# Layernorms with a full-matrix variance and a root on all partitions; the gelus of a feed-forward issued together

## The chip, the cores and the metric

The kernel runs on one core of one Trainium2 chip. The metric is the time of one execution on the device, in microseconds (us). A profile of one execution is at hand: it lists every instruction with its start and its length on each engine. The engines are TensorE (PE for matmuls, PEld for weight loads), VectorE (DVE), ScalarE (ACT), GpSimd (POOL) and SyncE (SP), which only issues DMAs here.

## What is computed

All data are fp32. The input x is 8 batches of 256 positions with 128 features; ctx is a second input of the same shape. The reference does, in short:

```
x1 = LN(x + ssm(x))            # LN, up-projection, conv of 4, silu, scan over 16 states, gate, down-projection
x2 = LN(x1 + cross(x1, ctx))   # layernorms, 16 heads of 64, softmax
x3 = x2
for 6 layers:
    x3 = x3 + attention(shift_tokens(x3))   # 16 heads of 64, windows of 32, normalised q and k, rotary tables
    x3 = x3 + ffn(shift_tokens(x3))         # LN(g, b); W1 128 -> 2 x 341; a * gelu(gate) @ W2
out = LN(x2 + x3)
LN(x) = (x - mean(x)) / sqrt(var(x) + 1e-5), over the 128 features, with g and b in some places
```

## The kernel before

Features lie on the 128 partitions and positions on the free axis. Two batches make a pair of 512 columns (`TP`), and there are four pairs. A matrix product on fp32 data runs as two passes on TensorE, so the profile counts two MATMUL records for each call. The kernel has three stages, one after the other, and a tail:

- Stage 1 (0 to 405 us of the span): the scan block, pair by pair. A generator `pre` prepares pair p + 1 (its layernorm included) while `scan` works on pair p.
- Stage 2 (405 to 770): cross-attention, pair by pair, with layernorms of the context, of x1 and of the result.
- Stage 3 (770 to about 2509): six layers of window attention and feed-forward.
- The tail, to 2556.5: the last feed-forward, then four final layernorms one after the other, and the stores.

There are 48 layernorms of 128x512: 8 in stage 1, 12 in stage 2, 24 in stage 3 (one in each feed-forward) and 4 in the tail. All go through the generator `layernorm_steps`: the mean by one product with `mean_w`, a full 128x128 matrix of 1/128 (L104); `ln_xc` = x - mean on VectorE (L106); `ln_sq` = its square on ScalarE (L108); then a `yield`. Next comes the variance (L112): four products in which a 128-column block of `ln_sq` is the weight and one column of `mean_w` the moving operand, so that the variances of 512 positions land as 128x4, one position per partition. `inv_root` takes Ln (with 1e-5 as bias) and then Exp with the scale -0.5 on ScalarE, both on 128x4 (`ln_rs`, L89, the line of the helper). After a second `yield`, four products spread the roots over the partitions (`ln_bc`, L122): each has a column of `ln_rs`, repeated 128 times, as its weight and the identity as moving operand. VectorE multiplies `ln_xc` by `ln_bc` (L127, or L129 and L130 with g and b).

PSUM is taken from pools with two buffers for each tag: `big` is 128x1024, `s` and `o` are 128x512. The pool of the layernorms' tiles has two buffers as well.

ScalarE must have the right table of functions loaded. `load_table` (L93) loads the one that holds Ln and Exp and keeps that instruction in program order; `with_table` makes Ln and Exp follow it. Other functions such as gelu load their table where they first stand in ScalarE's order.

In stage 3 the order of TensorE's instructions is the order in which the program is written (`tc.manual_schedule` for that engine alone). The order on the other engines is chosen by the framework's scheduler when the program is built, within data dependencies and `tc.issue_after` hints.

The written order comes from a list `slots` that is run through once for each batch of a layer (a turn). A turn has four groups. Each group begins with `turn_weights` (pT_ps, L730, with its copy pT on ScalarE, L734), and then has `project_out` (y_ps, L774, and x, L779, on VectorE) in groups 1 and 3, or `value` (v_ps by the products of L602, with its copy on ScalarE, L639) in groups 2 and 4; `attend` (o_ps, L742, and `on`, L749, on VectorE); `scores` (s_ps, L699; mask added on VectorE, L707; max, L712; subtraction on POOL, L713; Exp on ScalarE is `weigh`); `add_weights` (sum and reciprocal on VectorE, L722 and L723); `root` (max of `ss` on VectorE, L634, then Ln and Exp to `rn` on ScalarE); `turn` (qkT_ps, L652, copied by ScalarE to qT, L659, or kz, L664); `turn_output` (oT_ps, L761, copied by ScalarE, L765); `query_key` (qk_ps, L602; `sq` on ScalarE, L614; `qk`, `rb` and `ss` on VectorE, L621, L622 and L626; an addition on POOL, L625); `normalise` (POOL, L645). `spread` issues the DMAs of `vz` on SP.

A feed-forward of a pair (two batches) is a generator too. It is advanced by one step at each slot marked "ff": four slots in an even turn and four in an odd one. These steps have names in what follows:

- E1: shifted copies `fxs` on ScalarE (L793, L794).
- E2: the layernorm's mean, `ln_xc`, `ln_sq`.
- E3: variance and root.
- E4: `ln_bc` and the two operations that make `fxn` on VectorE.
- O1: `up(1)`, three products to f_ps (L808): the first two share a buffer of the tag `big`, the third takes one of `s`. Gelus 1 and 2 (L821).
- O2, right behind `turn_weights` of group 2: gelu 3 and `load_table`.
- O3: `up(0)` (again L808) and `fh` on VectorE (L827).
- O4: `down`, three products to f2_ps (L833), and x on VectorE (L834).

There are 24 feed-forwards. Between O1 and O3, tag `big` is used by qkT_ps, f_ps, qk_ps and v_ps, in this order, through two buffers, so v_ps of group 2 takes the buffer of f_ps, and may write only once gelus 1 and 2 have read it.

Of the kernel before, what the change touches and what calls it, by code (L numbers as in the profile page):

```python
# [9 lines left out]
FP = mybir.dt.float32  # L10
AF = mybir.ActivationFunctionType
ALU = mybir.AluOpType
AX = mybir.AxisListType

P = 128
# [34 lines left out]
def decoder_kernel(ctx: ExitStack, tc: tile.TileContext, a: dict, out: bass.AP):  # L50
    nc = tc.nc
    V, A, G, T = nc.vector, nc.scalar, nc.gpsimd, nc.tensor
# [3 lines left out]
    lnp = ctx.enter_context(tc.tile_pool(name="lnp", bufs=2))  # L56
# [5 lines left out]
    def ps_big(name):  # L62
        return banks[-1].tile([P, 1024], FP, tag="big", name=name)

    def ps_s(name):
        return banks[-1].tile([P, 512], FP, tag="s", name=name)
# [4 lines left out]
    ident = keep.tile([P, P], FP, name="ident")  # L71
# [3 lines left out]
    mean_w = keep.tile([P, P], FP, name="mean_w")  # L75
    G.memset(mean_w, 1.0 / D)
    eps_t = keep.tile([P, 1], FP, name="eps_t")
    G.memset(eps_t, EPS)

    def col(name, i=0, n=P):  # L80
        o = _OFF[name] + i
        return cols[:n, o : o + 1]

    table = []

    def with_table(f, *args, **kw):

        with tc.issue_after(table[-1].ins) if table else ExitStack():
            return f(*args, **kw)  # L89

    def load_table():
        table.append(
            tc.keep_in_program_order(A.preload_act_table_set("natural_log_exp_and_others"))  # L93
        )

    def inv_root(dst, src, bias=0.0):

        with_table(A.activation, dst, src, AF.Ln, bias=bias)
        with_table(A.activation, dst, dst, AF.Exp, scale=-0.5)

    def layernorm_steps(x, dst, g=None, b=None, view=lambda t: t):

        mu = ps_s("ln_mu")
        T.matmul(mu, lhsT=mean_w, rhs=x, start=True, stop=True)  # L104
        xc = lnp.tile([P, TP], FP, name="ln_xc")
        V.tensor_tensor(xc, x, mu, ALU.subtract)  # L106
        sq = lnp.tile([P, TP], FP, name="ln_sq")
        A.activation(sq, xc, AF.Square)  # L108
        yield
        var = ps_s("ln_var")  # L110
        for j in range(4):
            T.matmul(  # L112
                var[:, j : j + 1], lhsT=sq[:, j * P : (j + 1) * P], rhs=mean_w[:, 0:1],
                start=True, stop=True,
            )
        rs = lnp.tile([P, 4], FP, name="ln_rs")
        inv_root(rs, var[:, 0:4], eps_t)
        yield

        bc = ps_s("ln_bc")  # L120
        for j in range(4):
            T.matmul(  # L122
                bc[:, j * P : (j + 1) * P], lhsT=rs[:, j : j + 1].to_broadcast([P, P]), rhs=ident,
                start=True, stop=True,
            )
        if g is None:
            V.tensor_tensor(dst, xc, bc, ALU.mult)  # L127
        else:
            V.scalar_tensor_tensor(dst, view(xc), g, view(bc), ALU.mult, ALU.mult)  # L129
            V.tensor_scalar(dst, dst, b, None, ALU.add)  # L130

    def layernorm(*args):
        for _ in layernorm_steps(*args):
            pass
# [27 lines left out]
    with (  # L162
# [29 lines left out]
        def decay():  # L192
            with_table(A.activation, aa, cols[:, _OFF["a_log"] : _OFF["a_log"] + 2 * NS], AF.Exp)
            V.tensor_scalar(aa, aa, -1.0, None, ALU.mult)
            V.reciprocal(ia, aa)
            i_ps = ps_s("i_ps")
            for h in range(2):
                T.transpose(i_ps[:NS, h * P : (h + 1) * P], ia[:, h * NS : (h + 1) * NS], ident)
            A.copy(iaT.rearrange("n h p -> n (h p)"), i_ps[:NS, : 2 * P])
# [3 lines left out]
        for h in range(2):  # L203
            r_ps = ps_s("tap_ps")
            for k in range(KC):
                T.matmul(
                    r_ps[:, k * P : (k + 1) * P],
                    lhsT=col("conv_w", h * KC + k).to_broadcast([P, P]), rhs=ident,
                    start=True, stop=True,
# [16 lines left out]
        def pre(p, got, t_in=None):  # L226
# [7 lines left out]
            yield  # L234
            xn = xns[p % 2][:, :, KC - 1 :]
            yield from layernorm_steps(x, xn, col("ssm_g"), col("ssm_b"), two)
            yield
            xm, gate, dt = [], [], []
# [153 lines left out]
    with tc.tile_pool(name="s2w", bufs=1) as wp, tc.tile_pool(name="s2", bufs=2) as sp:  # L392
# [10 lines left out]
        def project(p, got):  # L403

            ct = sp.tile([P, TP], FP, name="ct")
            load_transposed(a["ctx_1024"], p, ct, sp)
            cn = sp.tile([P, TP], FP, name="cn")
            yield from layernorm_steps(ct, cn, col("ctx_w"), col("ctx_b"))
            yield
            la = sp.tile([P, TP], FP, name="la")  # L410
# [80 lines left out]
        for p in range(NPAIR):  # L491
# [13 lines left out]
            for hb in range(NHB):  # L505
                T.matmul(
                    y_ps, lhsT=wo[:, hb, :], rhs=oT[:, hb, :], start=(hb == 0), stop=(hb == NHB - 1)
# [7 lines left out]
    with ExitStack() as st:  # L515
# [270 lines left out]
        def feed_forward(d, p):  # L786

            w1, w2 = wts[d][1:3]
            x = x3[p]
            xs = sp.tile([P, 2, S], FP, name="fxs", bufs=1)  # L790
            x4 = x.rearrange("p (b s) -> p b s", b=2)
            G.memset(xs[HD:, :, 0:1], 0.0)
            A.copy(xs[:HD], x4[:HD])  # L793
            A.copy(xs[HD:, :, 1:], x4[HD:, :, : S - 1])  # L794
            xn = sp.tile([P, TP], FP, name="fxn", bufs=1)
            yield
            yield from layernorm_steps(
                xs.rearrange("p b s -> p (b s)"), xn, col("ff_g", d), col("ff_b", d)
            )
            yield  # L800
            hh = sp.tile([P, 3, TP], FP, name="fh", bufs=1)

            def up(i):

                pr, p2 = ps_big("f_ps"), ps_s("f_ps")
                got = []
                for dst, (f0, n) in zip((pr[:, :TP], pr[:, TP:], p2), FB):
                    T.matmul(  # L808
                        dst[:n], lhsT=w1[:, i * DFF + f0 : i * DFF + f0 + n], rhs=xn,
                        start=True, stop=True,  # L810
                    )
                    got.append(dst[:n])
                return got

            gts = []
            for j, g in enumerate(up(1)):
                n = FB[j][1]
                if j == 2:
                    yield
                gt = sp.tile([P, TP], FP, name="fg", bufs=3)  # L820
                A.activation(gt[:n], g, AF.Gelu, bias=col("ff_b1", d * 6 + 3 + j, n))  # L821
                gts.append(gt)
            load_table()
            yield
            for j, v in enumerate(up(0)):
                n = FB[j][1]
                V.scalar_tensor_tensor(  # L827
                    hh[:n, j, :], v, col("ff_b1", d * 6 + j, n), gts[j][:n], ALU.add, ALU.mult
                )
            yield  # L830
            y_ps = ps_s("f2_ps")
            for j, (f0, n) in enumerate(FB):
                T.matmul(y_ps, lhsT=w2[:n, j, :], rhs=hh[:n, j, :], start=(j == 0), stop=(j == 2))  # L833
            V.scalar_tensor_tensor(x, y_ps, col("ff_b2", d), x, ALU.add, ALU.add)  # L834
            yield
# [28 lines left out]
        def run(n):  # L864
            nonlocal ff
            for f, k, *args in slots:
                if f == "ff":
                    if k == n % 2:
                        next(ff, None)
                elif 0 <= n + k < len(seq):  # L870
                    f(n + k, *args)
                    if f is project_out and k < 0 and seq[n + k][1] % 2:
                        ff = feed_forward(seq[n + k][0], seq[n + k][1] // 2)
# [6 lines left out]
        with tc.manual_schedule(engines={mybir.EngineType.PE}):  # L880
            shift(0)
            for n in range(-2, len(seq)):
                run(n)
            project_out(len(seq) - 1, 1)
            for _ in feed_forward(DEPTH - 1, NPAIR - 1):
                pass
# [90 lines left out]
```

## Time and profile before

| | |
|---|---|
| Time, three runs | 2563.87, 2559.03, 2560.82 us; median 2560.82 |
| Profiled execution | 2558.4 us, its span 2556.5 us |
| PE busy | 2342.5 us, 92% of the span |
| PEld busy | 1469.9 us, 57% |
| DVE busy | 1800.3 us, 70% |
| ACT busy | 1468.3 us, 57% |
| POOL busy | 1428.2 us, 56% |
| DMA | 154.62 MB |
| granted TensorE clock, mean | 0.954 of full speed |

The span runs from the first to the last instruction in the profile; the execution's own time also has what lies before and after. Busy times of different engines overlap. A matmul's busy time may hold some waiting in TensorE's pipeline, and PEld overlaps PE. In lines of the profile, `a<-b,c 128x512` is the output, the inputs and the tile; `x8` counts records that are folded into one line; `[0.17 <-ACT pT L734]` is idle time of the engine ahead of the instruction and what ended it. The chain that ended last is followed back from the last instruction, at each step to what released it.

### The profile page before, as it was taken

The numbers are of one execution on the slowest core, as the hardware profiler recorded it, in microseconds if no ns is written. First come the engines' busy times: TensorE is split into PE (matmuls) and PEld (weight loads), VectorE is DVE, ScalarE is ACT, GpSimd is POOL, SyncE is SP. The second block draws the span as 40 slices with busy tenths as digits, with TensorE's granted clock in tenths as the row PEclk, the third lists the DMA queues.
The fourth block names the chain that finished last, engine by engine and source line by source line (L and its number), as shares of the span: only waits on it lengthen the run. The fifth ranks groups of instructions, "written<-read, shape, count | busy, mean of one in ns | idle before, by whom it ended". The sixth has DMA issues, their size and how long they took to land.

```text
span 2556.5 us, 54468 instructions
## 1 busy us (share of the span) xinstructions
PE 2342.5 (92%) x21378; PEld 1469.9 (57%) x21378; DVE 1800.3 (70%) x2671; ACT 1468.3 (57%) x2392; POOL 1428.2 (56%) x1174
## 2 busy tenths in 40 slices
PE   7687777999978999999999999999999999999996
PEld 3233224555445666666666666666666666666664
DVE  5777782544358778777778778777788777777762
ACT  4443422544435666666666666666666666666652
POOL 4877781322237655566656666566656656666630
PEclk8887877999989999999999999999999999999997
DMA  3433331000022223322232223222232223222220
GB/s 105 101 84 91 92 91 50 1 1 1 1 76 55 64 55 73 73 63 56 59 78 66 64 59 73 69 66 57 57 80 65 64 57 73 56 57 56 57 56 17
DMA packets 437962, 154.62 MB, mean 60 GB/s; under 512 B 401294, under 2 KB 417548, under 8 KB 437580
## 3 DMA queue, kind: packets, MB, share of 16 engines
q1 hardware_dynamic: 437708, 151.14, 24.4%
q8 instruction: 171, 2.80, 0.5%
q14 instruction: 83, 0.68, 0.1%
HBM read 55.33 MB, written 1.31 MB: 22 GB/s over the span
## 4 chain that ended last, share of the span: by engine, by line
DVE 27%; PE 26%; ACT 13%; POOL 1%; issue 1%; DMA 1%; SPq 1%; ACTq 0%; DVEq 0%; POOLq 0%
DVE qk L621 6%; DVE rb L622 6%; DVE ss L626 6%; PE qk_ps L602 5%; PE f_ps L808 3%; DVE on L749 3%; PE o_ps L742 3%; PE f_ps L833 2%; ACT sq L614 2%; PE qkT_ps L652 2%; DVE mx L722 2%; ACT kz L664 2%; PE s_ps L699 2%; PE oT_ps L761 2%; PE v_ps L602 2%; ACT pw L89 2%
## 5 line engine op out<-in xcount | busy, mean ns | idle before, releaser
L625 POOL TENSOR_TENSOR qk<-qk,rb 128x512 f32<-128x512 f32 x384 | 480.8, 1273 | 433.4 <-DVE rb L622 287.2
L645 POOL TENSOR_TENSOR qk<-qk,rn 128x1024 f32<-128x1024 f32 x192 | 369.0, 1922 | 31.0 <-ACT rn L89 28.7
L621 DVE TENSOR_TENSOR qk<-qk_ps,tab 128x1024 f32<-128x1024 f32 x192 | 234.8, 1223 | 204.2 <-ACT sq L614 204.2
L602 PE MATMUL qk_ps<-wqkv,xs 128*128 128x512 f32 x768 | 370.1, 605 | 7.3 <-issue 3.4
L713 POOL TENSOR_TENSOR pw<-pw,mx 128x512 f32<-128x512 f32 x192 | 200.1, 1042 | 160.5 <-DVE mx L712 106.8
L664 ACT COPY kz<-qkT_ps 64x1024 f32<-64x1024 f32 x192 | 193.4, 1007 | 118.5 <-PE qkT_ps L652 113.3
L742 PE MATMUL o_ps<-vz,pT 128*32 128x128 f32 x6144 | 207.5, 276 | 29.9 <-ACT pT L734 27.1
L626 DVE TENSOR_REDUCE ss<-sq 128x16 f32<-128x1024 f32 x192 | 232.0, 1208 | 3.2 <-ACT sq L614 3.2
L622 DVE TENSOR_TENSOR rb<-qk_ps,tab 128x1024 f32<-128x1024 f32 x192 | 233.0, 1214 | 1.4 <-POOL qk L625 1.4
L307 PE MATMUL y<-mc,ident 128*128 128x512 f32 x256 | 170.3, 768 | 66.5 <-POOL mc L326 63.3
L722 DVE TENSOR_REDUCE mx<-pw 128x8 f32<-128x512 f32 x192 | 130.6, 680 | 140.7 <-ACT pw L89 138.5
L461 POOL TENSOR_TENSOR ws<-w 128x512 f32<-128x512 f32 x64 | 81.3, 1270 | 259.7 <-ACT w L89 178.7
L742 PEld LDWEIGHTS o_ps<-vz,pT 128*32 128x32 f32 x6144 | 156.0, 109 | 118.4 <-ACT pT L734 107.5
L659 ACT COPY qT<-qkT_ps 128x1024 f32<-128x1024 f32 x96 | 97.2, 1012 | 218.5 <-PE qkT_ps L652 218.0
L614 ACT ACTIVATE sq<-qk_ps 128x1024 f32<-128x1024 f32 x192 | 195.3, 1017 | 41.2 <-PE qk_ps L602 35.0
L652 PE MATMUL qkT_ps<-ident,qk 128*128 128x128 f32 x1536 | 210.2, 280 | 7.3 <-POOL qk L645 4.3
L324 DVE TENSOR_TENSOR_SCAN m<-dw,ab 128x256 f32<-128x256 f32 x256 | 161.9, 670 | 59.5 <-POOL mc L326 37.8
L699 PE MATMUL s_ps<-kz,qT 128*32 128x128 f32 x6144 | 202.9, 273 | 0.6 <-ACT kz L664 0.6
L326 POOL TENSOR_TENSOR mc<-m,rows 128x512 f32<-128x512 f32 x128 | 167.9, 1318 | 53.2 <-PE d_ps L267 28.1
L602 PEld LDWEIGHTS qk_ps<-wqkv,xs 128*128 128x128 f32 x768 | 133.4, 194 | 104.4 <-issue 101.0
L652 PEld LDWEIGHTS qkT_ps<-ident,qk 128*128 128x128 f32 x1536 | 165.2, 141 | 48.3 <-issue 41.6
L774 PE MATMUL y_ps<-oT,wo 128*128 128x128 f32 x1536 | 187.7, 275 | 1.5 <-DVE ln_xc L106 0.9
(152 smaller groups left out, 4425.5 us busy)
## 6 DMA issues: line engine op xcount, KB each, us to landing
vz<-v SPq DMA_DIRECT2D x1152, 64.0 KB, 2.2
rows<-bc_dram SPq DMA_DIRECT2D x128, 256.0 KB, 3.7
vz<-v SPq DMA_DIRECT2D x576, 32.0 KB, 2.2
wqkv<-in_L_ffn_Wqkv SPq DMA_DIRECT2D x18, 512.0 KB, 4.7
wo<-in_L_ffn_Wo SPq DMA_DIRECT2D x6, 512.0 KB, 7.9
w<-in_L_ffn_W SPq DMA_DIRECT2D x6, 341.0 KB, 3.4
t_in<-in_x SPq DMA_DIRECT2D x4, 256.0 KB, 2.9
wkv<-in_L_xattn_Wkv SPq DMA_DIRECT2D x1, 1024.0 KB
```

The source lines that it names most:

```text
L602: T.matmul(pr[:, i * 512 : (i + 1) * 512], lhsT=got[n]["xs"][:, tb * P : (tb + 1) * P], rhs=thirds[seq[n][0], c][:, i * 512 : (i + 1) * 51 ...
L614: A.activation(sq, p3, AF.Square)
L621: V.tensor_tensor(t, p3, cs, ALU.mult)
L622: V.tensor_tensor(rb, p3, sn, ALU.mult)
L625: G.tensor_tensor(t[:, :, o], t[:, :, o], rb[:, :, f], ALU.add)
L626: V.tensor_reduce(got[n]["ss"][:, 2 * c + tb, :], sq, AX.X, ALU.add)
L645: G.tensor_tensor(t, t, r, ALU.mult)
L652: T.transpose(t_ps[:, hb * P : (hb + 1) * P], t[:, 2 * hb : 2 * hb + 2, :].rearrange("p h d -> p (h d)"), ident,)
L664: A.copy(kzs[0][r, :, e, W + tb * P : W + (tb + 1) * P], t3[r])
L699: T.matmul(s_ps[i * W : (i + 1) * W, j * P : (j + 1) * P], lhsT=qT[:, 4 * g + i, j * W : (j + 1) * W], rhs=kz[:, 4 * g + i, :, k0 : k0 + 2 ...
L713: G.tensor_tensor(pw, pw, mx[:, 0].unsqueeze(3).to_broadcast(shape), ALU.subtract)
L742: T.matmul(o_ps[i * W : (i + 1) * W, j * P : (j + 1) * P], lhsT=pT[:, j, i * W : (i + 1) * W], rhs=vz[:, j, i].rearrange("p e d -> p (e d) ...
```

## The change

The variance is one product with the full matrix `mean_w`, so that all 128 partitions hold the variance of each position, in a tile of 128x512. `inv_root` runs on that whole tile (Ln from PSUM into `ln_sq`, Exp in place), and `ln_bc` is gone: VectorE multiplies `ln_xc` by `ln_sq`. In `feed_forward`, the `yield` that stood ahead of gelu 3 stands ahead of gelu 1, so that all three gelus are written in step O2. They are issued through a new helper, `other_table`, which puts each behind the last four activations that went through `with_table` in ScalarE's order. The generator has as many steps as before.

```diff
-    table = []
+    table, recent = [], []
     def with_table(f, *args, **kw):
         with tc.issue_after(table[-1].ins) if table else ExitStack():
+            recent.append(f(*args, **kw))
+            return recent[-1]
+
+    def other_table(f, *args, **kw):
+        with ExitStack() as st:
+            for i in recent[-4:]:
+                st.enter_context(tc.issue_after(i.ins))
             return f(*args, **kw)
...
         A.activation(sq, xc, AF.Square)
         yield
         var = ps_s("ln_var")
-        for j in range(4):
-            T.matmul(
-                var[:, j : j + 1], lhsT=sq[:, j * P : (j + 1) * P], rhs=mean_w[:, 0:1],
-                start=True, stop=True,
-            )
-        rs = lnp.tile([P, 4], FP, name="ln_rs")
-        inv_root(rs, var[:, 0:4], eps_t)
+        T.matmul(var, lhsT=mean_w, rhs=sq, start=True, stop=True)
+        inv_root(sq, var, eps_t)
         yield
-        bc = ps_s("ln_bc")
-        for j in range(4):
-            T.matmul(
-                bc[:, j * P : (j + 1) * P], lhsT=rs[:, j : j + 1].to_broadcast([P, P]), rhs=ident,
-                start=True, stop=True,
-            )
         if g is None:
-            V.tensor_tensor(dst, xc, bc, ALU.mult)
+            V.tensor_tensor(dst, xc, sq, ALU.mult)
         else:
-            V.scalar_tensor_tensor(dst, view(xc), g, view(bc), ALU.mult, ALU.mult)
+            V.scalar_tensor_tensor(dst, view(xc), g, view(sq), ALU.mult, ALU.mult)
             V.tensor_scalar(dst, dst, b, None, ALU.add)
...
             for j, g in enumerate(up(1)):
                 n = FB[j][1]
-                if j == 2:
+                if j == 0:
                     yield
                 gt = sp.tile([P, TP], FP, name="fg", bufs=3)
-                A.activation(gt[:n], g, AF.Gelu, bias=col("ff_b1", d * 6 + 3 + j, n))
+                other_table(A.activation, gt[:n], g, AF.Gelu, bias=col("ff_b1", d * 6 + 3 + j, n))
                 gts.append(gt)
             load_table()
             yield
```

## The prediction

> **What bounds the kernel now.** I read the page first, then the busy time by stage, then ScalarE's and TensorE's timelines over one period of the window-attention stage, then the chain that ended last.
>
> ```profile
> span 2556.5 us, 54468 instructions
> ...
> PE 2342.5 (92%) x21378; PEld 1469.9 (57%) x21378; DVE 1800.3 (70%) x2671; ACT 1468.3 (57%) x2392; POOL 1428.2 (56%) x1174
> ...
> DVE 27%; PE 26%; ACT 13%; POOL 1%; issue 1%; DMA 1%; SPq 1%; ACTq 0%; DVEq 0%; POOLq 0%
> ```
>
> PE is busy 92% of the span, yet the chain has as much VectorE as TensorE in it: the bound alternates. Busy time by stretch (columns: stretch, length, then PE, PEld, DVE, ACT, POOL busy with counts, clock, DMA share, GB/s):
>
> ```profile
> 860.00:2480.00 1620.00, 1562.33 (x17797) 1084.52 (x17796) 1263.69 (x1891) 1063.72 (x1747) 979.02 (x781) 1.00 0.27 64
> ...
> 1492.96:1564.73 71.77, 69.38 (x790) 48.11 (x789) 55.74 (x84) 47.45 (x78) 43.83 (x36) 1.00 0.24 56
> ```
>
> Stage 3 is 24 feed-forwards at about one per 71.8 us (E1 to E4, O1 to O4, as named above); 22 of them run in this steady state. In the chain, O3, O4 and E1 go through PE without a gap; E2 to O1 go through sq -> qk, rb, ss on DVE and back through ACT. So a cycle gets longer wherever either link does. ScalarE's timeline across O1 and O2 (start, length, instruction, idle before it):
>
> ```profile
> 1548.54 1.28 ACT L821 ACT_TABLE_LOAD   x1
> 1549.83 1.26 ACT L821 ACTIVATE fg<-f_ps,cols 128x512 f32<-128x512 f32 x2
> 1550.98 0.58 ACT L765 COPY oT<-oT_ps 128x512 f32<-128x512 f32 x1
> 1551.45 0.70 ACT L821 ACTIVATE fg<-f_ps,cols 85x512 f32<-85x512 f32 x1
> 1552.03 1.02 ACT L614 ACTIVATE sq<-qk_ps 128x1024 f32<-128x1024 f32 x1
> 1552.93 0.59 ACT L734 COPY pT<-pT_ps 128x512 f32<-128x512 f32 x1
> 1553.55 1.28 ACT L93 ACT_TABLE_LOAD   x1
> ```
>
> Today sq waits behind all three gelus, although its input left PE at about 1551.3. TensorE's timeline, same stretch:
>
> ```profile
> 1537.98 1.06 PE L122 MATMUL ln_bc<-ident,ln_rs 128*128 128x128 f32 x8
> 1538.87 0.60 PE L761 MATMUL oT_ps<-ident,on 128*128 128x128 f32 x4
> ...
> 1551.09 0.60 PE L730 MATMUL pT_ps<-ident,pw 128*128 128x128 f32 x4
> 1551.52 1.88 PE L602 MATMUL v_ps<-wqkv,xs 128*128 128x512 f32 x4
> 1553.58 1.08 PE L742 MATMUL o_ps<-vz,pT 128*32 128x128 f32 x32 [0.17 <-ACT pT L734]
> ...
> 1557.22 0.66 PE L761 MATMUL oT_ps<-ident,on 128*128 128x128 f32 x4 [0.57 <-DVE on L749]
> ...
> 1559.43 0.60 PE L730 MATMUL pT_ps<-ident,pw 128*128 128x128 f32 x4
> ```
>
> v_ps starts right behind pT_ps: the slot it takes, that of up(1)'s first two products, is free because gelus 1 and 2 ended at 1551.09. Last, the chain in the tail, where each layernorm stands alone:
>
> ```profile
> 2536.72 1.88 PE ln_var L112 x8
> ...
> 2538.62 0.27 ACT ln_rs L89
> ...
> 2539.18 2.08 PE ln_bc L122 x8
> 2541.26 1.72 PE ln_mu L104 x2
> ```
>
> **What the Trainium skill says.** "PSUM — Partial Sum Buffer", section "Engine vs sequencer instructions": ScalarE's and VectorE's queues are strict FIFO and matmuls start in program order; the timelines agree (sq idle behind the gelus). The same page, "PSUM bank collisions raise a hardware error": two engines on one bank get a dependency, ACT and DVE too; that is why DVE's qk waited 204.2 us in all on ACT's sq. "TensorE: Matmul & The Clock Gate", "What's actually happening": after an idle window the array runs at half clock; here ln_mu takes 1.02 us at 1520.23 and 2.07 at 218.87.
>
> **The change, part by part.** 48 layernorms.
>
> *Variance.* Removed per layernorm: 8 ln_var passes and 8 ln_bc passes; 0.91 + 0.89 us of PE in steady state (start to start), 1.88 + 2.08 where PE is cold. Added: two passes of 512 columns, priced by ln_mu, which has the same form: 0.86 warm, 2.07 cold.
>
> *Root.* Removed on ACT: 0.26 and 0.20 us. Added: Ln of 128x512 out of PSUM and Exp of 128x512, absent before: nearest rows are the gelu at 0.69 and the pw Exp at 0.63; "ScalarE: Activation LUTs", "What ACT_TABLE_LOAD costs", gives about 280 ns + 0.833 ns per element, 0.71 us as an estimate. I take 0.69 + 0.69 (ends 1.2 and 1.5). No table load is added: both built programs have 74.
>
> *Exposed layernorm.* Cold: -1.88 -0.55 -2.09 +2.07 +1.43 = about -1.0 us; warm -0.4 to -2. Beyond this, PE no longer holds the next layernorm behind ln_bc, so ln_mu starts while the root runs.
> - Tail: four in a row, 7.7 us apart (2525.8, 2533.5, 2541.3). New spacing: mu 1.75 + xc 0.75 + sq 0.67 + var 2.1 = 5.3. Two spacings give 4.8; the first and the way to the stores about 2.5 more; the last feed-forward's own 1.1: -8.4. The drain before it loses a PE-bound ln_bc: -0.9.
> - Stage 1 to 2 (399.89 to 425.04: three layernorms in line): following each link, the first pr moves from 425.04 to about 420: -5.
> - Stage 1: at each pair boundary t_ps and s_ps come after ln_bc on PE, and POOL waits for y (5.95 us at 236.02). About 1.5, 1.5 and 2.5 off, 0.4 at the start, and 1.5 from ln_bc (1.91 cold at 247.57) leaving PE during a scan: -7.5. POOL's work bounds the rest.
> - Stage 2 is PE-bound: nine layernorms, -0.7 for six in the loop, -1.5 for three at pair ends: -8.7.
>
> Sum outside stage 3: -30.5 us (-23 to -36).
>
> *Stage 3.* The two built programs give each engine's order. PE gains 0.05 in E3 and 0.89 in E4, but E4 is on the DVE-ACT link, so this opens a PE gap and saves nothing; were PE the link there, it would be worth 22 x 0.9 = 20 us. I follow the link with the durations above, in the old times.
> 1. E3: fxn's two DVE operations (0.73 + 0.71) move here, ahead of the softmax sum; they wait for Exp (end 1532.2) and end at 1533.7, where the sum started at 1533.49: +0.17.
> 2. E4: sq moves ahead of the pw Exp, pitch 0.53: -0.53. DVE's qk of O1 starts at 1542.68 instead of 1543.04.
> 3. O1: the softmax sum (0.6), the max (0.6) and the reciprocal now precede the small ss operation on DVE: ss ends 6.2 us after qk instead of 5.0. ACT's two rn and the gelu table load queue behind it: load at 1549.41 instead of 1548.54.
> 4. O2, the edit of the gelus: ACT's order becomes load, gelu 1, oT, sq, pT, gelu 2, gelu 3, load. Load 1.29, gelu 0.57, oT 0.47: sq at 1551.74, 0.3 earlier. But v_ps needs gelu 2: sq 0.90, pT 0.49, gelu 0.69: v_ps at 1553.88 instead of 1551.52. Behind v_ps on PE queue o_ps, s_ps, qkT_ps, oT_ps, qk_ps and the next pT_ps, 6.79 us back to back: O3's pT_ps at 1560.67 instead of 1559.43.
>
> So +1.24 us per cycle: old idle (0.25 + 0.12 + 0.70 in O2) is used up, and a new PE wait of 2.7 takes its place. DVE's "on" ends at 1557.6 and is no longer what oT_ps (1558.5) waits for. O3 and O4 are PE-bound, so nothing wins it back. 22 x 1.24 = 27, less about 1 where a weight DMA sets E3's end (5 cycles): +26 us (+16 to +36). The DMA issue that moves on SP (one weight load past one vz) is early by many us: nothing.
>
> **Sum.** -30.5 + 26 = -4.5 us on the profiled execution's 2558.4 (span 2556.5): 2553.9. The median of the three runs is 2.4 above that execution, so I say 2556. No-change cannot be told from a difference within 0.2%, about 5.1 us.
>
> **Rivals.**
> - *The gelu wait wins; slower.* The v_ps wait is the one of step 4; from 1.39 us per cycle on it outweighs the rest, from 1.62 it is slower by 0.2%. O2 has little reserve: ACT's sq in O2 comes 0.37 after PE's qk_ps, and O3's o_ps has 0.2 us to spare on pT. With 0.6 us more on ACT there, 1.9 x 22 = 42: +11, 2572. For it: ACT's queue is dense from the load to kz. Against: every step has a measured pitch.
> - *The wait is mostly hidden; faster.* If the scheduler's new DVE order costs less than the 1.2 us of step 3 (rn ready in time), v_ps comes 0.9 earlier: 0.35 x 22 = 8: -23, 2538. For it: the pw Exp and POOL leave slack in O1. Against: ss is fourth behind "on" in the new order.
> - *The edit does not do what it says.* In the built order only gelus 2 and 3 are adjacent; this is in the forecast already.
>
> **How the numbers follow.** Forecast as worked out, net -14 to +5: chance 0.55, of it 0.26 faster by over 0.2%, 0.28 within, 0.01 slower; wait wins 0.23; wait hidden 0.22. Hence faster 0.26 + 0.22 = 0.48, within 0.2% 0.28, slower 0.23 + 0.01 = 0.24. The forecast's own range is 2547 to 2565; to leave no more than 2 in 10 out, 2541 to 2572.
>
> **What would show it.** Right: v_ps in O2 starts some 2.3 us after the pT_ps that precedes it and names ACT fg; the cycle is near 73.0; the tail's layernorms stand 5.3 apart; the first pr starts near 412 (stage 1 being shorter as well). Wrong: a cycle still at 71.8 (step 3 or 4 fails), a cycle above 73.5, or a tail that is not shorter by 7 us. A PE clock below 1.00 in stage 3, from the new gap in O2, would make all of stage 3 longer than this sum.

## The result and the profile after

The changed kernel takes 2625.14 us (median of four runs, 2617.31 to 2627.97) against 2559.93 us for the kernel before (now four runs, 2555.01 to 2563.87). The ratio is 1.0251, with a 95% interval from 1.0222 to 1.028: it is slower by 2.5%. The forecast was 2556 us with a range from 2541 to 2572, so it was wrong, in sign and in size.

The profiled execution took 2617.3 us, 58.9 more than the one of before. It is the fastest of the four; the others, at a mean clock of 0.944 or 0.945 instead of 0.950, took 7 to 11 us more, so what follows divides up 59 us and not the 65 between the medians. The head of its page:

```profile
span 2615.1 us, 53126 instructions
...
PE 2317.5 (89%) x20706; PEld 1395.0 (53%) x20706; DVE 1832.0 (70%) x2671; ACT 1507.4 (58%) x2392; POOL 1435.5 (55%) x1174
...
PE 32%; DVE 24%; ACT 12%; SPq 1%; issue 1%; DMA 1%; POOL 0%; ACTq 0%; DVEq 0%; POOLq 0%
```

PE has 25 us less to do, and PE's share of the chain has risen from 26% to 32%: PE waits and runs slowly on the path, where it did little of either before. DVE is 32 us busier although it does the same operations.

The start of the first feed-forward (its first `fxs`) and of the last one cut both spans into three parts:

| | before | after | difference | forecast |
|---|---|---|---|---|
| start to first fxs (stages 1 and 2, start of 3) | 863.40 | 838.49 | -24.9 | -21.2 |
| first fxs to last fxs (23 feed-forwards) | 1635.90 | 1733.51 | +97.6 | +26 |
| last fxs to the end (drain and tail) | 57.2 | 43.1 | -14.1 | -9.3 |
| span | 2556.5 | 2615.1 | +58.6 | -4.5 |

So the gain outside stage 3 is there, and larger than forecast. The loss lies in stage 3: the middle cycle is 76.28 us instead of 71.76, that is 4.5 more, where 1.24 were forecast. I lay one cycle of after (from its fxs at 1528.32) over one of before (from 1512.30) and compare the starts of TensorE's groups. All are within 0.1 us up to qkT_ps of E4. Then three steps come:

- oT_ps of E4: +1.35, of which 1.21 is left at O1.
- v_ps of O2: another 2.69, to +3.90.
- o_ps behind it: another 1.45, to +5.35. At oT_ps 0.8 of this is won back, since `on` had been awaited there before. The cycle stays 4.5 longer.

**E4.** VectorE's timeline of after, and then GpSimd's:

```profile
1547.01 0.69 DVE L709 TENSOR_REDUCE mx<-pw 128x8 f32<-128x512 f32 x1
1548.44 0.93 DVE L126 SCALAR_TENSOR_TENSOR fxn<-ln_xc,cols,ln_sq 128x512 f32<-128x512 f32 x1 [0.74 <-ACT ln_sq L89]
1549.40 2.01 DVE L127 TENSOR_SCALAR fxn<-fxn,cols 128x512 f32<-128x512 f32 x1
1551.33 0.67 DVE L719 TENSOR_REDUCE mx<-pw 128x8 f32<-128x512 f32 x1
...
1555.51 0.68 DVE L746 TENSOR_TENSOR on<-o_ps,mx 128x512 f32<-128x512 f32 x1
```

```profile
1547.78 1.05 POOL L710 TENSOR_TENSOR pw<-pw,mx 128x512 f32<-128x512 f32 x1 [0.73 <-DVE mx L709]
1548.78 2.35 POOL L642 TENSOR_TENSOR qk<-qk,rn 128x1024 f32<-128x1024 f32 x1
```

The operation that adds b to fxn (L127) takes 2.01 us. It ends at 1551.41, 0.28 after normalise on POOL (1548.78 + 2.35 = 1551.13). Normalise itself is longer than its usual 1.90, and it started while fxn's first operation was under way. In the kernel before, the same operation met a shorter one on POOL:

```profile
1540.71 0.71 DVE L130 TENSOR_SCALAR fxn<-fxn,cols 128x512 f32<-128x512 f32 x1
1540.10 1.04 POOL L713 TENSOR_TENSOR pw<-pw,mx 128x512 f32<-128x512 f32 x1 [0.70 <-DVE mx L712]
```

It ended at 1541.42, again 0.28 after POOL's operation (1540.10 + 1.04 = 1541.14). In the last feed-forward, where POOL has nothing to do, it takes 0.49 in both kernels. So the 0.71 of before held a wait for POOL already. The Trainium skill, "SBUF — State Buffer", section "Who interferes with whom", says that VectorE and GpSimd share one pair of SBUF ports, that a `tensor_scalar` with both operands in SBUF can take the pair, as can a VectorE operation with two SBUF inputs against a GpSimd one that reads SBUF, and that the one which issues second "fully blocks". The numbers agree. The change gave fxn's first operation a second SBUF input (`ln_sq`, where `ln_bc` was in PSUM), and it moved both operations to where POOL runs normalise instead of the subtraction. The price falls on `on`, which stands in VectorE's order behind all this; oT_ps on TensorE waits 2.06 us for it.

**O2.** ScalarE's timeline of after, and then TensorE's:

```profile
1566.94 1.28 ACT L97 ACT_TABLE_LOAD   x1
1568.23 0.69 ACT L97 ACTIVATE fg<-f_ps,cols 128x512 f32<-128x512 f32 x1
1568.82 0.58 ACT L762 COPY oT<-oT_ps 128x512 f32<-128x512 f32 x1
1569.29 1.04 ACT L611 ACTIVATE sq<-qk_ps 128x1024 f32<-128x1024 f32 x1
1570.20 0.60 ACT L731 COPY pT<-pT_ps 128x512 f32<-128x512 f32 x1
1570.67 1.28 ACT L97 ACTIVATE fg<-f_ps,cols 128x512 f32<-128x512 f32 x2
```

```profile
1568.32 0.60 PE L727 MATMUL pT_ps<-ident,pw 128*128 128x128 f32 x4
1571.44 3.57 PE L599 MATMUL v_ps<-wqkv,xs 128*128 128x512 f32 x4 [2.53 <-ACT fg L97]
1574.94 1.14 PE L739 MATMUL o_ps<-vz,pT 128*32 128x128 f32 x32
```

Gelu 2 is behind sq and pT, and v_ps waits for it, as forecast. What was not in the sum is that v_ps then takes 3.57 us instead of 1.88. The busy time of that stretch (columns: stretch, length, PE, PEld, DVE, ACT and POOL busy with counts, clock, DMA share, GB/s) says why:

```profile
1571.40:1576.80 5.40, 5.36 (x68) 2.70 (x68) 3.77 (x6) 3.47 (x4) 2.49 (x2) 0.68 0.00 2
1576.80:1580.00 3.20, 3.20 (x25) 2.12 (x18) 1.57 (x5) 2.41 (x4) 2.37 (x2) 1.00 0.29 47
```

The mean clock granted is 0.68 of full speed for 5.4 us after the wait: half speed for 3.41 us of them, then full speed. Such a stretch at half clock is called a clock drop in what follows. "TensorE: Matmul & The Clock Gate", section "What's actually happening", gives half clock after an idle window of about 3.4 us that runs freely; here a wait of 2.5 us was enough. The same can happen after the wait in E4. TensorE's timeline of after, one cycle in which it did:

```profile
1171.71 0.65 PE L758 MATMUL oT_ps<-ident,on 128*128 128x128 f32 x4 [2.06 <-DVE on L746]
1172.20 3.48 PE L599 MATMUL qk_ps<-wqkv,xs 128*128 128x512 f32 x4
```

qk_ps takes 3.48 here and 1.88 in the cycle above, behind the same wait of 2.06 us. The clock's records in the trace tell the two apart. All 27 clock drops in stage 3 of after are 3.41 us long, and all begin on one grid of 3.41 us; call one step of it a window. In the window ahead of each drop TensorE stands without a matmul for 1.9 to 2.5 us, and no other window in stage 3 has more than 2.0. Here are the window of the wait above and the next one, and then the two windows that share the wait of the cycle that starts at 1528.32 (columns as above):

```profile
1168.91:1172.32 3.41, 1.35 (x12) 1.11 (x11) 3.41 (x5) 1.01 (x1) 2.25 (x2) 1.00 0.22 35
1172.32:1175.74 3.42, 3.42 (x7) 1.25 (x6) 0.87 (x2) 2.04 (x5) 2.72 (x3) 0.50 0.58 95
1551.20:1554.61 3.41, 2.98 (x73) 2.54 (x72) 3.38 (x6) 2.11 (x4) 0.10 (x2) 1.00 0.09 16
1554.61:1558.03 3.42, 1.79 (x8) 1.07 (x9) 3.11 (x5) 1.46 (x3) 2.72 (x3) 1.00 0.43 67
```

In the first pair the whole wait lies in one window, and the next one runs at half clock. In the second a boundary cuts the wait, and the clock stays full. So a cycle pays or not according to where its wait falls on the grid. Of the 22 cycles 11 have a drop in E4 (1.7 us each at O1) and 16 one in O2; this is why they scatter from 75.5 to 77.5.

### The profile page after: what moved, and what is told of

Same layout as the page of the kernel before. It is cut to its first block, busy times and chain, and to the rows that moved or that the text cites. A ratio compares the mean times of both kernels' runs of the same rounds, so it can differ in the third digit from the quotient of the medians.

```text
span 2615.1 us, 53126 instructions
## 1 busy us (share of the span) xinstructions
PE 2317.5 (89%) x20706; PEld 1395.0 (53%) x20706; DVE 1832.0 (70%) x2671; ACT 1507.4 (58%) x2392; POOL 1435.5 (55%) x1174
## 3 DMA queue, kind: packets, MB, share of 16 engines
q1 hardware_dynamic: 437708, 151.14, 30.5%
## 4 chain that ended last, share of the span: by engine, by line
PE 32%; DVE 24%; ACT 12%; SPq 1%; issue 1%; DMA 1%; POOL 0%; ACTq 0%; DVEq 0%; POOLq 0%
PE qk_ps L599 6%; DVE qk L618 5%; DVE rb L619 5%; DVE ss L623 5%; PE v_ps L599 4%; PE o_ps L739 4%; PE qkT_ps L649 3%; PE f_ps L805 3%; PE s_ps L696 3%; PE y_ps L771 2%; PE f_ps L830 2%; ACT sq L611 2%; DVE mx L719 2%; PE oT_ps L758 2%; DVE fxn L127 2%; DVE on L746 1%
## 5 line engine op out<-in xcount | busy, mean ns | idle before, releaser
L642 POOL TENSOR_TENSOR qk<-qk,rn 128x1024 f32<-128x1024 f32 x192 | 375.2, 1954 | 54.5 <-ACT rn L89 52.6
L599 PE MATMUL qk_ps<-wqkv,xs 128*128 128x512 f32 x768 | 382.1, 622 | 10.2 <-issue 3.6
L599 PE MATMUL v_ps<-wqkv,xs 128*128 128x512 f32 x384 | 199.9, 646 | 48.5 <-ACT fg L97 48.5
L739 PE MATMUL o_ps<-vz,pT 128*32 128x128 f32 x6144 | 215.3, 283 | 23.6 <-ACT pT L731 23.5
L739 PEld LDWEIGHTS o_ps<-vz,pT 128*32 128x32 f32 x6144 | 161.5, 112 | 120.6 <-ACT pT L731 80.8
```

What stands on the lines that cost most here:

```text
L599: T.matmul(pr[:, i * 512 : (i + 1) * 512], lhsT=got[n]["xs"][:, tb * P : (tb + 1) * P], rhs=thirds[seq[n][0], c][:, i * 512 : (i + 1) * 51 ...
L642: G.tensor_tensor(t, t, r, ALU.mult)
L739: T.matmul(o_ps[i * W : (i + 1) * W, j * P : (j + 1) * P], lhsT=pT[:, j, i * W : (i + 1) * W], rhs=vz[:, j, i].rearrange("p e d -> p (e d) ...
```

## The experiments

The theory (A) was now: the length of E4 is the shared port; the length of O2 is the place of gelus 2 and 3; each wait is made dearer by TensorE's clock; and outside stage 3 the new layernorm is a gain. The kernels below are timed against the kernel before on the same chip; ratios are with 95% intervals. "Shift" is the start of a TensorE group in one cycle against the cycle of before.

**The gelus alone.** On the kernel before, with the helper `other_table` as in the change:

```diff
-                if j == 2:
+                if j == 0:
                     yield
...
-                A.activation(gt[:n], g, AF.Gelu, bias=col("ff_b1", d * 6 + 3 + j, n))
+                other_table(A.activation, gt[:n], g, AF.Gelu, bias=col("ff_b1", d * 6 + 3 + j, n))
```

> The edit of the gelus alone, on the old layernorms. Theory A (gelus hurt only where the scheduler puts gelu 2 behind sq and pT): in this program ScalarE's order is load, gelu 1, oT, gelu 2, gelu 3, sq, pT, so v_ps of O2 is late by about the 0.5 us of oT and sq by nothing; cycle 71.8 to 72.8, time 2560 to 2580 against 2560. Rival B (issuing the gelus in step O2 costs whatever the layernorms are): v_ps waits some 2.7 us, cycle near 75, time near 2630.

Measured: 2558.54 us, ratio 0.9995 (0.9986 to 1.0003); the middle cycle is 71.79. ScalarE's timeline of this kernel in O2:

```profile
1186.99 0.69 ACT L97 ACTIVATE fg<-f_ps,cols 128x512 f32<-128x512 f32 x1
1187.58 0.58 ACT L773 COPY oT<-oT_ps 128x512 f32<-128x512 f32 x1
1188.05 1.26 ACT L97 ACTIVATE fg<-f_ps,cols 128x512 f32<-128x512 f32 x2
1189.20 1.02 ACT L622 ACTIVATE sq<-qk_ps 128x1024 f32<-128x1024 f32 x1
```

The gelus stand ahead of sq, v_ps is late by 0.13 us (0.5 expected), and the cycle gains and loses nothing. The same edit costs nothing on the old layernorms and much on the new ones: it is the order that the scheduler makes of it that costs.

**All three gelus early.** On the changed kernel, the step of O2 holds `load_table` alone:

```diff
             for j, g in enumerate(up(1)):
                 n = FB[j][1]
-                if j == 0:
-                    yield
                 gt = sp.tile([P, TP], FP, name="fg", bufs=3)
                 other_table(A.activation, gt[:n], g, AF.Gelu, bias=col("ff_b1", d * 6 + 3 + j, n))
                 gts.append(gt)
+            yield
             load_table()
```

> The changed kernel with all three gelus written in O1, so ScalarE's order is load, gelus 1 to 3, oT, sq, pT. Theory A: the wait of v_ps on fg and the slow v_ps behind it go, worth 3.3 us per cycle; the 1.2 us of E4 stay, as does some of the later ss in O1; cycle 73 to 73.5, time near 2552 (2545 to 2562) against 2625 of the changed kernel. Rival B (the whole of the 4.5 us comes from VectorE's new order, and the gelu wait only sits where the lateness shows): the cycle stays above 75, time above 2600.

Measured: 2587.30 us, ratio 1.0094 (1.0064 to 1.0124), 38 us less than the changed kernel and 35 more than I expected. In a cycle without a clock drop (74.15 us) the shifts are 1.22 in E4 and then 0.79 at v_ps and 0.39 at o_ps, so O2's loss has gone from 3.3 to 1.2. But most cycles are 75.2 to 75.3, so B's cycle above 75 came true, though not for B's reason: after E4's wait the groups from qk_ps on run slowly, 1.7 us in all at O1. All 15 clock drops in stage 3 of this trace come in E4, where the changed kernel has 11 there; none is left in O2.

**The root and fxn's product in PSUM.** On the changed kernel:

```diff
-        inv_root(sq, var, eps_t)
+        inv_root(var, var, eps_t)
...
-            V.tensor_tensor(dst, xc, sq, ALU.mult)
+            V.tensor_tensor(dst, xc, var, ALU.mult)
...
-            V.scalar_tensor_tensor(dst, view(xc), g, view(sq), ALU.mult, ALU.mult)
-            V.tensor_scalar(dst, dst, b, None, ALU.add)
+            V.scalar_tensor_tensor(view(var), view(xc), g, view(var), ALU.mult, ALU.mult)
+            V.tensor_scalar(dst, view(var), b, None, ALU.add)
```

> The changed kernel, but the root is written to PSUM in place of ln_var and the first product of fxn too, so that neither of fxn's two VectorE operations has two SBUF inputs or reads and writes SBUF alone. Theory A (the 1.2 us in E4 are the shared SBUF port of VectorE and GpSimd: fxn's last operation waits for POOL's normalise to end): that operation takes 0.7 us instead of 2.0, the wait of oT_ps on `on` in E4 goes from 2.06 to below 0.9, the cycle shortens by 1.0 to 1.4 us, time 2595 to 2605. Rival B (E4 is late because fxn's two operations stand ahead of the softmax sum in VectorE's order, whatever their length): the cycle stays near 76.3 and the time near 2625.

Measured: 2556.20 us, ratio 0.9982 (0.9974 to 0.9989): 69 us less than the changed kernel, where 20 to 30 were expected. VectorE's timeline in E4:

```profile
1155.15 0.76 DVE L126 SCALAR_TENSOR_TENSOR ln_var<-ln_xc,cols,ln_var 128x512 f32<-128x512 f32 x1 [0.61 <-ACT ln_var L89]
1155.94 0.75 DVE L127 TENSOR_SCALAR fxn<-ln_var,cols 128x512 f32<-128x512 f32 x1
1156.61 0.68 DVE L719 TENSOR_REDUCE mx<-pw 128x8 f32<-128x512 f32 x1
```

Normalise ran on POOL from 1155.62 for 1.90 us, that is, at the same time; both operations keep their length. They stand ahead of the sum here too, so it is not their place as such: E4 is 0.46 us *early* at O1, where it was 1.21 late: 1.67 us a cycle, or 37 us. Most of the rest is clock: no drop is left in E4 (11 in the changed kernel), and 12 are in O2 (16 there). Outside stage 3 nothing moved: the first fxs stands at 839.3 instead of 838.5, and the tail takes 43.4 us instead of 43.1. O2 keeps its wait for gelu 2 and often its clock drop: nine of the 22 cycles are 72.6 us, most others 74.2, and of two that I laid side by side the short one has a shift of 1.70 at o_ps, the long one 2.75.

**The root alone in PSUM.** On the changed kernel; the product goes to SBUF and the addition stays there (one execution, so without an interval):

```diff
-        inv_root(sq, var, eps_t)
+        inv_root(var, var, eps_t)
...
-            V.scalar_tensor_tensor(dst, view(xc), g, view(sq), ALU.mult, ALU.mult)
+            V.scalar_tensor_tensor(dst, view(xc), g, view(var), ALU.mult, ALU.mult)
```

> The changed kernel with the root in PSUM, so that fxn's first operation has one SBUF input; its second operation still reads and writes SBUF alone. Theory A (the second one is what waits for POOL's normalise; the first one only held normalise up): the first takes 0.73 instead of 0.93 us, normalise starts 0.4 earlier, the second still lasts until normalise ends, 1.5 to 1.9 us, and E4 is 0.8 to 0.9 us late instead of 1.35. Rival B (two SBUF inputs of the first are the whole matter): the second takes 0.7 us and E4 is as in the run with both in PSUM, 0.3 us early.

Measured: 2595.65 us beside 2560.66. Both operations of fxn in this kernel, by name of the tile (minimum, median and maximum in ns):

```profile
L126 DVE SCALAR_TENSOR_TENSOR fxn<-ln_xc,cols,ln_var x24: 746/748/749, 859.5 to 2555.9; 128x512 f32<-128x512 f32 x24
L127 DVE TENSOR_SCALAR fxn<-fxn,cols x24: 486/1871/1895, 860.3 to 2556.7; 128x512 f32<-128x512 f32 x24
```

The first is at its old length, the second still waits; E4's shift at oT_ps is 0.90. So about a third of E4's 1.35 is the first operation, which holds normalise up, and the rest the second, which then waits for normalise.

**The old place of fxn in VectorE's order.** On the changed kernel:

```diff
-    table, recent = [], []
+    table, recent, last_max = [], [], []
...
-            V.scalar_tensor_tensor(dst, view(xc), g, view(sq), ALU.mult, ALU.mult)
-            V.tensor_scalar(dst, dst, b, None, ALU.add)
+            with tc.issue_after(last_max[-1].ins) if last_max else ExitStack():
+                V.scalar_tensor_tensor(dst, view(xc), g, view(sq), ALU.mult, ALU.mult)
+                V.tensor_scalar(dst, dst, b, None, ALU.add)
...
-            V.tensor_reduce(mx[:, 0], pw, AX.X, ALU.max)
+            last_max.append(V.tensor_reduce(mx[:, 0], pw, AX.X, ALU.max))
```

> The changed kernel with fxn's two VectorE operations kept behind the max of E4's group, where the kernel before has them; their operands stay in SBUF. Theory A (the port: the last of them waits for whatever POOL instruction is under way): it again takes over 0.7 us when it meets POOL, but the softmax sum and `on` of E4 are no longer behind it, so oT_ps of E4 is on time; E4's 1.2 us and its clock drops go, O2's wait stays; time 2570 to 2600. Rival B (the length of fxn is what counts, wherever it stands): as late as the changed kernel, above 2615.

Measured: 2576.06 us, ratio 1.0062 (1.0041 to 1.0082). oT_ps of E4 is 0.31 us early (0.33 with both in PSUM), although the operands are in SBUF and the second operation takes 1.15 us, ending again 0.28 after POOL's subtraction. `on` is no longer behind them. E4's loss needs both: the operations ahead of the sum *and* the port. O2 loses 3.3 as before (shift 2.92 at its end).

**Work for TensorE in O2's wait.** On the changed kernel, three products whose result nobody reads:

```diff
                 if j == 0:
                     yield
+                    warm = ps_o("warm")
+                    for _ in range(3):
+                        T.matmul(warm, lhsT=mean_w, rhs=xn, start=True, stop=True)
```

> The changed kernel with three products of 128x512 that nobody reads, put on TensorE in O2 between pT_ps and v_ps, where it waits for gelu 2. Theory A (v_ps and o_ps run slow there because TensorE's clock drops in the wait): v_ps starts at the same distance from pT_ps, takes 1.9 us instead of 3.5, the cycle shortens by about 1.4 us, time near 2593. Rival B (v_ps is slow because its second half waits for something, a bank or gelu 3): v_ps still takes 3.5 us, time 2620 to 2630.

Measured: 2591.54 us, ratio 1.0121 (1.0097 to 1.0145), 34 us *less* than the changed kernel with more work. TensorE's timeline in O2:

```profile
1101.33 0.60 PE L727 MATMUL pT_ps<-ident,pw 128*128 128x128 f32 x4
1101.77 2.74 PE L819 MATMUL warm<-fxn,mean_w 128*128 128x512 f32 x6
1104.45 1.98 PE L599 MATMUL v_ps<-wqkv,xs 128*128 128x512 f32 x4
1106.37 1.08 PE L739 MATMUL o_ps<-vz,pT 128*32 128x128 f32 x32
```

v_ps starts 3.12 us after pT_ps, exactly as in the changed kernel, and takes 1.98 instead of 3.57. Of the 1.69 us that the slow v_ps lost, 1.59 are gone, so it was the clock; six clock drops are left in stage 3, all in E4.

**Both repairs.** Early gelus and PSUM together (the diffs of both, above):

> The changed kernel with both repairs: gelus 1 to 3 written in O1, and the root and fxn's first product in PSUM. Theory A (the port costs E4, the place of gelus 2 and 3 costs O2, and a drop of TensorE's clock after each of these waits makes them dearer): E4 as in the run with PSUM alone (0.5 us below before), O2 as in the run with early gelus (1.2 us above), cycle 72.4 to 72.8 without a clock drop, time 2530 to 2545. Rival B (the two repairs take away the same loss, because a start that is late in E4 is what makes O2 late): no better than PSUM alone, 2550 to 2560.

Measured: 2524.77 us, ratio 0.9866 (0.9849 to 0.9882), below both expectations. The middle cycle is 72.10: E4 -0.45, O2 +0.79, and no clock drop is left in stage 3. The losses are separate and nearly add up: 38 and 69 us less than the changed kernel for each repair alone, 100 for both. O2 keeps a rest.

**The Exp of pw one group earlier.** On the kernel with both repairs:

```diff
-    table, recent = [], []
+    table, recent, last_exp = [], [], []
...
-            A.activation(sq, p3, AF.Square)
+            first = c == 1 and tb == 0 and n % 2 == 0 and last_exp
+            with tc.issue_after(last_exp[-1].ins) if first else ExitStack():
+                A.activation(sq, p3, AF.Square)
...
-            with_table(A.activation, pw, pw, AF.Exp)
+            last_exp.append(with_table(A.activation, pw, pw, AF.Exp))
...
-            (turn_weights, 0, 0), (weigh, 0, 1), (project_out, -1, 1),
+            (turn_weights, 0, 0), (project_out, -1, 1),
...
-            (turn_output, 0, 3), (query_key, 2, k, 0), (normalise, 2, q, 1),
+            (turn_output, 0, 3), (weigh, 1, 1), (query_key, 2, k, 0), (normalise, 2, q, 1),
```

> As the kernel with both repairs, and the Exp of pw that belongs to the group of O1 is traced one group earlier, with sq of E4 kept behind it, so that VectorE has the softmax sum and reciprocal done before qk of O1 and ss stands ahead of the max, as in the kernel before. Theory A (the late ss of O1, 1.2 us, is what is left of the loss in O2): the gelu table load comes 0.9 us earlier, O2's loss goes from 1.2 to below 0.3, cycle 71.3 to 71.7, time 2508 to 2522. Rival B (O2's loss comes from oT and sq standing behind three gelus): O2 still loses about 1.2 us, time 2530 to 2545.

Measured: 2509.29 us, ratio 0.9806 (0.9791 to 0.9822). The middle cycle is 71.38, and O2's shift is zero beyond E4's -0.4. TensorE's timeline in O2:

```profile
1162.34 0.60 PE L729 MATMUL pT_ps<-ident,pw 128*128 128x128 f32 x4
1162.78 1.88 PE L599 MATMUL v_ps<-wqkv,xs 128*128 128x512 f32 x4
1164.83 1.08 PE L741 MATMUL o_ps<-vz,pT 128*32 128x128 f32 x32 [0.17 <-ACT pT L733]
```

This is the pattern of before. With ss ahead of the max again, the table load and the gelus are on time. This kernel beats both: 1.9% below before, 4.4% below the changed kernel (2509.29 / 2625.14 = 0.956).

**The new layernorm outside stage 3 only.** On the kernel before, which gets the new `layernorm_steps` beside the old one under another name; its gelus stay as they are:

```diff
-            yield from layernorm_steps(
+            yield from layernorm_old(
                 xs.rearrange("p b s -> p (b s)"), xn, col("ff_g", d), col("ff_b", d)
             )
```

> The new layernorm in stages 1 and 2 and in the tail only; the 24 feed-forwards keep the old layernorm and the old place of the gelus. Theory A (the change is a gain outside stage 3: 25 us up to the first fxs, 14 in the tail): stage 3 as in the kernel before, 72.1 us a cycle, time 2518 to 2526. Rival B (part of the gain outside is given back in stage 3 whatever stands there, for instance by a later load of weights): above 2530.

Measured: 2527.78 us, ratio 0.9877 (0.9862 to 0.9892), 32 us below before and just above A's range. Start to first fxs -20.9, stage 3 +1.7, tail -11.0. So the gain outside is real and not given back in stage 3, but 32 us where the changed kernel has 39. Three of the missing us are the tail's clock, which was lower again in part (below); the other four lie ahead of the first fxs, which stands anywhere between 836 and 845 us in the kernels here that have the new layernorm. That goes with the clock in stages 1 and 2: the time at half clock ahead of the first fxs is 157 to 195 us in these traces, 164 in the one with the earliest first fxs and 195 in the one with the latest. Whether it is the cause was not tested.

**The new layernorm without the edit of the gelus.** On the changed kernel, and one execution:

```diff
-                if j == 0:
+                if j == 2:
                     yield
...
-                other_table(A.activation, gt[:n], g, AF.Gelu, bias=col("ff_b1", d * 6 + 3 + j, n))
+                A.activation(gt[:n], g, AF.Gelu, bias=col("ff_b1", d * 6 + 3 + j, n))
```

> The new layernorm alone: the gelus as in the kernel before, in their old place and without the helper that keeps them behind the activations of the other table. In this program's ScalarE order the Ln and Exp of rn stand between the gelus, with 162 table loads instead of 74: four more in each feed-forward. Theory A (they lie on the way to sq and v_ps in O2): 22 x 4 x 1.28 = 113 us more than the run with early gelus, less what was idle there: 2660 to 2710. Rival B (the loads hide behind TensorE's work): 2580 to 2600.

Measured: 2666.92 us beside 2560.66. ScalarE's timeline in O1:

```profile
1194.82 1.28 ACT L818 ACT_TABLE_LOAD   x1
1196.12 0.69 ACT L818 ACTIVATE fg<-f_ps,cols 128x512 f32<-128x512 f32 x1
1196.82 1.28 ACT L89 ACT_TABLE_LOAD   x1
1198.12 0.21 ACT L89 ACTIVATE rn<-ss 128x16 f32<-128x16 f32 x1
1198.35 1.28 ACT L818 ACT_TABLE_LOAD   x1
```

The program has 162 table loads instead of 74, because the scheduler put gelus between the Ln and the Exp of rn; that it does so because rn comes late in VectorE's new order is likely and not shown. The helper of the change is what prevents this (next run, 74 loads); the two parts of the change belong together.

**The old place of the gelus, but through the helper.** On the changed kernel; one execution:

```diff
-                if j == 0:
+                if j == 2:
                     yield
```

> The changed kernel with the gelus' old place (1 and 2 in O1, 3 in O2), but through the helper. ScalarE's order is load, gelus 1 and 2, oT, sq, pT, gelu 3. Theory A (v_ps needs gelus 1 and 2 alone, and sq has one gelu fewer ahead of it): v_ps as in the run with early gelus, o_ps 0.5 us earlier, cycle 73.6 to 74.2 where no clock drop comes, time 2570 to 2590. Rival B (what counts is that the three stand together): between the changed kernel and early gelus, above 2595.

Measured: 2573.03 us beside 2560.66. The cycles are 73.5 to 75.3. In the undisturbed ones (73.6 us; shift 1.20 at O1) v_ps comes 0.79 later, as with early gelus, and o_ps wins 0.14 back, where early gelus lose another 0.39: as A has it. In the cycles that lose more to the clock in E4 (shift up to 2.90 at O1), v_ps is on time or at most 0.3 late. So of the change's two edits to the gelus the helper is needed, and the moved `yield` costs about 50 us here.

## Why the prediction was wrong

- **Outside stage 3: right, mis-sized in the tail.** Sum forecast -30.5, measured -39.0. The first pr stands at 410.0, where "near 412" was to be seen. Stage 2 and the rest up to the first fxs gave 9.9 (425.04 to 410.01 is 15.0 of the 24.9). The tail was forecast with PE cold, spacing 5.3 us; the timeline of after shows 3.4:

```profile
2595.21 1.02 PE L112 MATMUL ln_mu<-x,mean_w 128*128 128x512 f32 x2
2597.67 1.13 PE L120 MATMUL ln_var<-ln_sq,mean_w 128*128 128x512 f32 x2 [1.44 <-ACT ln_sq L116]
2598.64 1.02 PE L112 MATMUL ln_mu<-x,mean_w 128*128 128x512 f32 x2
```

  Both products run at full clock, where I priced 1.75 and 2.1. This is in part luck: in the ten other kernels with the new layernorm the last stretch is 43.4 to 46.2 us long, where it is 43.1 here, and in several of them the clock drops after the first of the four layernorms.
- **Step 1 of stage 3 (E3): the step that failed first.** It priced fxn's two operations at 0.73 + 0.71 from the rows of before and let them end at 1533.7 of the old time. They took 0.93 + 2.01. The 0.71 was not the operation's own length (0.49 where POOL is idle) but its wait for a short operation on POOL; I moved it next to normalise, which is nearly twice as long, and did not look at what POOL does there, nor at the page of the skill on the shared ports. This is +1.2 us per cycle at O1 instead of about nothing, and in 11 of the 22 cycles another 1.7 of clock drop.
- **Step 2 (E4): hidden by it.** qk of O1 was to start 0.36 earlier and started 1.16 later (31.90 against 30.74 after fxs). With PSUM, E4 is indeed 0.46 early.
- **Step 3 (O1): right.** ss ends 6.2 us after qk's start (1560.22 to 1566.43), as worked out. The kernel with the Exp of pw one group earlier shows what it is worth: it takes 15 us off (2524.77 to 2509.29).
- **Step 4 (O2): right in mechanism and in its first size.** v_ps starts 3.12 us after pT_ps, 2.69 more than before; forecast 2.36 more. What failed is the end of the step: v_ps to the next pT_ps was taken as "6.79 us back to back" at full speed. It took 8.53 (43.12 to 51.65 after fxs), because the clock fell in the wait; with TensorE kept busy in the wait it took 6.9. I had named this as what would make all of stage 3 longer, and put no price on it. The trace of before had one. In two of its 22 cycles, both of 74.2 us, the clock drops after a short wait in E3; TensorE's timeline of the first:

```profile
1313.09 1.05 PE L112 MATMUL ln_var<-mean_w,ln_sq 128*128 128x1 f32 x8 [1.22 <-DVE x L779]
1314.00 0.63 PE L761 MATMUL oT_ps<-ident,on 128*128 128x128 f32 x4
1314.47 3.52 PE L602 MATMUL qk_ps<-wqkv,xs 128*128 128x512 f32 x4
```

  Here too qk_ps takes 3.52 us instead of 1.88. (The forecast's sign, v_ps "some 2.3 us after the pT_ps", was its lateness against before, where v_ps starts 0.43 after pT_ps already.)
- **Sum of one cycle:** 1.21 (E4) + 2.69 (wait) + 1.45 (clock) - 0.84 (old idle used up) = 4.51; 22 cycles make 99, and 97.6 were measured over the 23 intervals. This is the middle cycle, with a clock drop in O2 alone; seven of the 22 are of that kind, and the others lose 3.8 to 5.7.
- **The rivals.** "The gelu wait wins; slower" had the right wait and the right sign; its point of decision, 1.39 us per cycle, was passed three times over. It was priced by more work on ScalarE, which was not what came.

## What to carry to other kernels

When an operation moves on VectorE, do not take its old duration along: look at what GpSimd does in its new place and at which of its operands are in SBUF; keeping one operand in PSUM made the two engines run side by side here. A wait of 2 us that you put in front of TensorE can cost more than the wait, since the products behind it can run slowly; price it, or fill it. And read an edit of issue order from the built program as a whole: here the edit of the gelus was worth 0 on the old layernorm; on the new one its moved `yield` cost about 50 us, and leaving the whole edit out cost another 42.

## What was not expected of the hardware

- TensorE's clock fell after waits of 2.06 and 2.53 us, in some cycles and not in others of the same program. What decides in the trace of after is how much of one window of 3.41 us is idle, and so where the wait falls. The idle time in the profile is not the whole measure: in the kernel before a window with 1.22 us of it was followed by a drop, with the eight passes of ln_var, of one column each, in the same window. Products of no use, 2.74 us of them, in the wait kept the clock, for a gain of 34 us.
- In the tail a single core at the same pattern of work ran at different clocks. The kernel before has 0.63 over its four last layernorms; the changed kernel runs them at 1.00 although TensorE is idle for 1.44 of each 3.4 us; with the new layernorm outside stage 3 only, ln_mu took 1.91, 1.70 and 1.02 us one after the other. The windows show where these two part: behind the first of the four, one with 1.96 us idle is followed by full clock in the changed kernel, and one with 1.97 by half clock in the other. In the kernel before, the clock, once at half, came back only after a nearly full window: those with 0.6 to 1.4 us idle were followed by half clock again, and the one with 0.41 by full clock. No run was made to test this.
